# Message products with stationary weights, turned by VectorE, in a graph network layer on one Trainium2 core

## The chip, the cores and the metric

The kernel runs on one core of one Trainium2 chip. A core has five engines that run their own instruction streams: PE (matrix products), DVE (vector), ACT (activations), POOL (here it issues the gathers) and SP (here it issues other transfers). The metric is the device time of one execution in microseconds; lower is better. The kernel before took 5120.48 us, the median of 3 runs (5115.68 to 5129.49).

## The reference

One layer of a graph network with N = 12500 nodes, C = 96 channels and E = 412500 edges that have 4 attributes each. The edges come sorted by dst.

```python
def _mlp(h, W, b, gamma, beta):
    h = jax.nn.relu(h @ W + b)
    mu = jnp.mean(h, axis=0)
    var = jnp.mean(jnp.square(h - mu), axis=0)
    return gamma * (h - mu) * jax.lax.rsqrt(var + EPS) + beta

node_feat = _mlp(x, W_node, ...)
edge_feat = _mlp(edge_attr, W_edge, ...)
message = jnp.concatenate([x[row], x[col], edge_feat], axis=1)   # row = src, col = dst
message = _mlp(message, W_msg, ...)
agg = segment_sum(message, col, N)
out = _layernorm(x + agg + node_feat)
```

The norm of the messages is over all edges, so that the kernel needs, of the relu'd messages h, the sums by dst (with a count), the total and the total of squares; it applies the norm to the sums at the end.

## The kernel before, in words

The product with W_msg is split by its three parts. x @ W_src and x @ W_dst are computed once per node into two tables in DRAM, p_tab and q_tab (tables(), L180). A message is then relu(p_tab[src] + q_tab[dst] + edge part).

Edges are taken in tiles of 128 (one edge a partition), groups of GT = 4 tiles (512 edges) and blocks of BG = 4 groups (16 tiles). There are NT = 3223 tiles, NG = 806 groups and NBL = 202 blocks. As the edges are sorted by dst, the edges of a group fall on few nodes: a window of WN = 31 nodes, and the windows of the four groups of a block start WS = 16 nodes apart, so that a block covers NW - 1 = 79 nodes.

**Gathers.** gather() (L202) issues one indirect DMA per tile on POOL: 128 rows of 96 floats from p_tab, by src. In the first stages, in which tables, node MLP and the statistics of the edge norm are computed, POOL gathers the rows of the first 29 blocks ("early" ones) and SP writes them to DRAM (spill, blocks(), L217). The other 173 blocks ("late" ones) are gathered in the main loop, through a ring of 7 tiles of two groups each (RING = 14 groups); ahead_of() issues the four gathers of the group 14 ahead, and its tile comes free when the message() of the groups in it has read it. plan() (L91) mixes the blocks: about every sixth late block is followed by an early one, whose rows SP fetches back (fetch(), L572) and which needs no gather.

**The main loop** (L704 to L780, about 900 to 5066 us of the execution) goes over the groups k in that order. All its engines' orders are written out by hand: an engine executes what the loop names in the order of the loop. For a group:

- edges() (L599): a bf16 product of 512 columns with the edge attributes (split in bf16 parts) and, for the place of an edge in its window, a one-hot condition, into the PSUM tile pr, two groups at a time.
- prepare() (L608): ACT takes the relu of both groups (127 partitions x 1024) into left. left has for each edge, a column, 96 edge features, 31 rows that select the node in the window, and a row of ones.
- linear() (L615): for each of the 4 tiles, a fp32 product with 128 columns of left as the stationary side and rhs (96 rows of weights, 31 rows of q_tab, the bias; 96 columns) as the moving one. The result z has an edge a partition, 96 columns, and lies in one of three PSUM banks zb (ZB = 3).
- message() (L627): DVE adds the gathered rows to z, and takes the relu, into h (128 x 384).
- squared() (L648): ACT squares two groups of h; moments() (L653) adds them on DVE into the PSUM tile mixed.
- places_of() (L639): once per block DVE compares the place of each edge with the 31 numbers of its group's window; the result, at, is the one-hot of 128 edges x 80 places (the 80th column is one, for the total).
- sums() (L672): per tile, a fp32 product with h (97 columns) stationary and the 80 columns of at moving, added up over a block in one of two PSUM banks by_place.
- add() (L695): DVE adds the bank to total and to agg at the block's first node, a block and 2 groups later.

An fp32 product shows in the trace as two weight loads (PEld) and two matmuls (PE). linear() works up to ZB - 1 = 2 groups ahead of message(), sums() LATER = 2 groups behind. Behind the loop come the statistics and the output (to 5104 us).

Of the kernel before, what the change touches and what calls it, by code (L numbers as in the profile page):

```python
# [26 lines left out]
P = 128  # L27
# [13 lines left out]
RW = 7  # L41
# [27 lines left out]
AB, HP, RB, ZB = 2, 3, 3, 3  # L69
NW = WS * (BG - 1) + WN + 1  # L70
OW = NW * GT + WS * (BG - 1)
# [36 lines left out]
def gnn(ctx, tc, t):  # L108
# [35 lines left out]
    iota = const.tile([P, BG, WN], F32, name="iota")  # L144
    nc.gpsimd.iota(iota, pattern=[[WS, BG], [1, WN]], base=-WM, channel_multiplier=0,
# [123 lines left out]
    with tc.tile_pool(name="win", bufs=1) as win, tc.tile_pool(name="win_ps", bufs=2, space=PSUM) as ps:  # L269
# [12 lines left out]
        worst = win.tile([P, 2, BG], F32, name="worst")  # L282
        for k in range(BG):
            nc.vector.tensor_reduce(worst[:, 0, k:k + 1], rel[:, k:NG:BG, :], axis=AX.XY, op=OP.max)
            nc.vector.tensor_reduce(worst[:, 1, k:k + 1], rel[:, k:NG:BG, :], axis=AX.XY, op=OP.min)
        out = win.tile([P, 1], F32, name="out")
        nc.vector.tensor_sub(worst[:, 0, :], worst[:, 0, :], iota[:, :, WN - 1])
        nc.vector.tensor_sub(worst[:, 1, :], iota[:, :, 0], worst[:, 1, :])
        nc.vector.tensor_reduce(out, worst.rearrange("p a k -> p (a k)"), axis=AX.X, op=OP.max)
# [29 lines left out]
    def places():  # L319

        with tc.tile_pool(name="lin", bufs=2) as work, tc.tile_pool(name="lin1", bufs=1) as one:
            first = one.tile([P, RW], I32, name="first")
            nc.sync.dma_start(first, t["first"])
            rows = [stack_d[HI + BG * i:HI + BG * (i + 1), :].rearrange("g (c b e) -> (g c) b e", b=RW, e=GE)
# [151 lines left out]
    def fast(ring):  # L476
        y0s, pair = [], [None]

        def ahead_of(g):
            if g % 2 == 0:  # L480
                pair[0] = ring.tile([P, 2, GT, C], F32, name="pg")
            if g < NG:
                return gather(g, pair[0][:, g % 2, :, :])

        with tc.manual_schedule(engines={ET.SP, ET.Pool}):
# [23 lines left out]
            got = {g: ahead_of(g) for g in range(SPILL, SPILL + RING)}  # L509
        with tc.tile_pool(name="fix", bufs=1) as fix, tc.tile_pool(name="msg", bufs=2) as work, \  # L510
                tc.tile_pool(name="msg_ps", bufs=2, space=PSUM) as ps:
            squares = fix.tile([P, C], F32, name="squares")
            mixed = ps.tile([P, GE], F32, name="mixed", bufs=1)
            wide_sq = mixed[:, :GT * C].rearrange("p (t c) -> p t c", c=C)
            nc.vector.memset(wide_sq, 0.0)
            nodes_of = mixed[:, GT * C:GT * C + BG * WN].rearrange("p (k w) -> p k w", w=WN)
            nc.vector.tensor_copy(nodes_of, iota)
            by_place = [ps.tile([P, GE], F32, name=f"pa{i}", bufs=1) for i in range(2)]
# [15 lines left out]

            at = [fix.tile([P, BG, OW], F32, name=f"at{i}") for i in range(AB)]
            for x in at:
                nc.vector.memset(x, 0.0)
                for i in range(BG):
                    o = WS * (BG - 1 - i)
                    nc.vector.memset(x[:, i, o:o + NW * GT].rearrange("p (t w) -> p t w", w=NW)[:, :, NW - 1:], 1.0)  # L540


            zb = [ps.tile([P, GE], F32, name=f"z{i}", bufs=1) for i in range(ZB)]
# [7 lines left out]
            def load(s):  # L551
# [16 lines left out]
                rows = bass.AP(rows.tensor, rows.offset, [[C, WN], [WS * C, BG], [1, C]], None, rows.runtime_checks)  # L568
# [3 lines left out]
            def fetch(s):  # L572
                b = order[s]
                if b * BG < SPILL:
                    back = work.tile([P, BG, GT, C], F32, name="pb", bufs=1)
                    nc.sync.dma_start(back, spill[b].rearrange("p g (a c) -> p g a c", a=GT))
                    for i in range(BG):
                        got[b * BG + i] = back[:, i, :, :]

            def unread(n):  # L580
                busy = ps.tile([P, 2, GE], F32, name="pr", bufs=1)[:, 0, :GE // 2]
                for i in range(n):
                    nc.tensor.matmul(busy, ident[:C], big[:C, -GE // 2:], start=True, stop=True)

            raw = {}

            def transposed(k):

                s, g = steps[k]
                px = ps.tile([P, 2, GE], F32, name="pr", bufs=1)  # L590
                for i in range(2):
                    for t in range(GT):
                        nc.tensor.transpose(px[:C, i, t * P:(t + 1) * P], got[g + i][:, t, :], ident)  # L593
                xt = work.tile([C, 2, GE], F32, name="xt", bufs=1)
                nc.scalar.activation(xt, px[:C], AF.Copy)  # L595
                for i in range(2):
                    raw[g + i] = xt[:, i, :]

            def edges(s, half):  # L599

                n = min(2, NG - order[s] * BG - 2 * half)
                if n > 0:
                    prs[s, half] = ps.tile([P, 2, GE], F32, name="pr", bufs=1)
                for i in range(n):
                    nc.tensor.matmul(prs[s, half][:, i, :], we[:, 2 * half + i, :], block[s],  # L605
                                     start=True, stop=True)

            def prepare(s, half):  # L608

                n = min(2, NG - order[s] * BG - 2 * half)  # L610
                if n > 0:
                    pr, x = prs.pop((s, half)), left[s % 2]
                    nc.scalar.activation(x[:C + WN, 2 * half:2 * half + n, :], pr[:C + WN, :n, :], AF.Relu)  # L613

            def linear(k):  # L615
                s, g = steps[k]
                n = min(GT, NT - g * GT)
                for i in range(n):
                    nc.tensor.matmul(zb[k % ZB][:, i * C:(i + 1) * C],  # L619
                                     left[s % 2][:KR, g % BG, i * P:(i + 1) * P],  # L620
                                     rhs[:KR, s % RB, g % BG, :], start=True,
                                     stop=g not in raw)
                    if g in raw:
                        nc.tensor.matmul(zb[k % ZB][:, i * C:(i + 1) * C], raw[g][:, i * P:(i + 1) * P],  # L624
                                         w_msg[:, 0, :], start=False, stop=True)

            def message(k):  # L627
                s, g = steps[k]
                n = min(GT, NT - g * GT)
                z = zb[k % ZB][:, :n * C].rearrange("p (t c) -> p t c", c=C)  # L630
                h = hb[k // 2 % HP][:, k % 2, :, :C]
                rows = got.pop(g)
                if g in raw:
                    nc.vector.tensor_scalar(h, z, 0.0, MOST, op0=OP.max, op1=OP.min)
                    return
                nc.vector._custom_dve(TENSOR_ADD_SAT, out=h[:, :n, :], in0=z, in1=rows[:, :n, :],  # L636
                                      s0=MOST, s1=0.0)

            def places_of(s):  # L639

                b = order[s] * BG
                o, m = WS * (BG - 1), min(BG, NG - b)
                to = at[s % AB][:, :m, o:o + NW * GT].rearrange("p g (t w) -> p g t w", w=NW)[:, :, :, :WN]
                nc.vector.tensor_tensor(  # L644
                    to, rel[:, b:b + m, :].unsqueeze(3).to_broadcast([P, m, GT, WN]),
                    nodes_of[:, :m].unsqueeze(2).to_broadcast([P, m, GT, WN]), op=OP.is_equal)

            def squared(k, m=2, n=GT):  # L648
                sq = work.tile([P, 2, GT, C], F32, name="sq")
                nc.scalar.activation(sq[:, :m, :n, :], hb[k // 2 % HP][:, k % 2:k % 2 + m, :n, :C], AF.Square)  # L650
                return sq

# [7 lines left out]
            def collect(x, n, r=P):  # L660

                plus = nc.gpsimd.tensor_add
                whole = n if r == P else n - 1
                if r < P:
                    plus(squares[:r], x[:r, whole * C:n * C], squares[:r])
                while whole > 1:
                    half = whole // 2
                    plus(x[:, :half * C], x[:, :half * C], x[:, (whole - half) * C:whole * C])
                    whole -= half
                plus(squares, x[:, :C], squares)  # L670

            def sums(k):  # L672
# [4 lines left out]
                o = WS * (BG - 1 - i)  # L677
                for t in range(n):
                    r = min(P, E - (g * GT + t) * P)
                    nc.tensor.matmul(by_place[s % 2][:C + 1, :NW], hb[k // 2 % HP][:r, k % 2, t, :],  # L680
                                     at[s % AB][:r, i, o + NW * t:o + NW * (t + 1)],
# [13 lines left out]
            def add(s, val):  # L695

                pt = by_place[s % 2][:C + 1, :NW]
# [7 lines left out]
            with tc.manual_schedule(engines={ET.SP, ET.Pool, ET.PE, ET.DVE, ET.Activation}):  # L705
                bad = nc.values_load(flag, min_val=0, max_val=1, skip_runtime_bounds_check_because="a comparison's result")
                load(0)
                fetch(0)
                load(1)
                fetch(1)  # L710
                for half in range(2):
                    edges(0, half)
                    prepare(0, half)
                edges(1, 0)
                for k in range(ZB - 1):
                    linear(k)
                places_of(0)
                waiting, last = None, BG * (len(order) - 1)
                for k in range(last):
                    s, g = steps[k]  # L720
                    if g % BG == 0:
                        if s + 2 < len(order):
                            load(s + 2)
                            fetch(s + 2)
# [320 lines left out]
```

## Time and profile before

| | |
|---|---|
| median of 3 runs | 5120.48 us |
| the profiled execution: its time, its span | 5105.89 us, 5104.1 us |
| mean granted clock of TensorE | 0.66 |
| the main loop | about 900 to 5066 us |
| largest group of ACT in the loop: relu, L613 | 403 x 1021 ns, 411.4 us |
| DMA traffic over the span | 317.20 MB, 62 GB/s |

The page of the profile gives each engine's busy time, a chart of 40 slices, the DMA queues, the chain that ended last and the costliest groups of instructions. A line such as `L613 ACT ACTIVATE left<-pr 127x1024 f32<-127x1024 f32 x403 | 411.4, 1021 | 2696.3 <-remote 2114.7` has the kernel's line, engine, operation, output and input with their shapes (partitions x elements), and the count; then the busy time of all and the mean duration of one in ns; then the idle time of the engine just before them, and what ended most of it. "issue" is time in which an engine waited for nothing that the profile shows. Of 40 slices, these show that from the seventh on the loop is even:

```profile
PE   3244443445555555555555655555555555555656
DVE  1457767222222222222222222222222222222224
POOL 4755555655556656666565666665666666656664
PEclk6557666666666666666666666666666666666667
```

### The profile page before, as it was taken

How to read it: one execution, taken by the hardware profiler on the slowest of the kernel's cores; microseconds unless marked ns; L12 is line 12 of the kernel's file. 1: busy time of each engine (PE TensorE's matmuls, PEld its weight loads, DVE VectorE, ACT ScalarE, POOL GpSimd, SP SyncE). 2: the span in 40 equal slices, each digit the busy share in tenths (PEclk: the TensorE clock that was granted, in tenths of full speed). 3: DMA queues.
4: the chain of work that ended last, by engine and by line, in shares of the span. 5: the costliest groups of instructions: out<-in, count | busy, mean ns of one | idle time of the engine just before them, and what ended most of it. 6: DMA issues, size and time to landing. Idle time of an engine off the chain costs nothing.

```text
span 5104.1 us, 43293 instructions
## 1 busy us (share of the span) xinstructions
PE 2651.1 (52%) x15169; PEld 2168.5 (42%) x15169; DVE 1575.8 (31%) x3039; ACT 1138.2 (22%) x1226; POOL 3088.9 (61%) x3248
## 2 busy tenths in 40 slices
PE   3244443445555555555555655555555555555656
PEld 3031111445444444444444544445444444444545
DVE  1457767222222222222222222222222222222224
ACT  0426554111111111111111211112111111111112
POOL 4755555655556656666565666665666666656664
PEclk6557666666666666666666666666666666666667
DMA  6734443221222222222222212222212222212122
GB/s 162 248 113 95 101 98 92 49 48 48 59 56 47 46 46 49 46 48 49 46 46 46 48 39 48 47 50 47 47 46 47 49 46 47 48 45 48 40 47 59
DMA packets 214865, 317.20 MB, mean 62 GB/s; under 512 B 126498, under 2 KB 132988, under 8 KB 211808
## 3 DMA queue, kind: packets, MB, share of 16 engines
q0 software_dynamic: 103040, 158.48, 14.7%
q1 hardware_dynamic: 98635, 150.92, 10.0%
q10 hardware_dynamic: 12960, 4.93, 0.4%
q8 instruction: 122, 2.00, 0.2%
q14 instruction: 108, 0.88, 0.1%
HBM read 258.19 MB, written 55.89 MB: 62 GB/s over the span
## 4 chain that ended last, share of the span: by engine, by line
PE 34%; issue 27%; another core or an unknown queue 17%; ACT 3%; DVE 2%; ACTq 0%; DVEq 0%
PE z L619 17%; PE pa L680 12%; PE pr L605 5%; ACT left L613 2%; ACT sq L650 1%; DVE estats L409 0%; DVE part L414 0%; PE z L624 0%; DVE h L636 0%; PE pr L593 0%; DVE y L968 0%; ACT xt L595 0%; DVE sd L971 0%; ACT sq L970 0%
## 5 line engine op out<-in xcount | busy, mean ns | idle before, releaser
L207 POOL DMA_INDIRECT pg<-p_tab,src x3156 | 3005.8, 952 | 1902.8 <-issue 893.4
L619 PE MATMUL z<-rhs,left 128*128 128x96 f32 x6446 | 1224.8, 323 | 788.0 <-issue 784.1
L619 PEld LDWEIGHTS z<-rhs,left 128*128 128x128 f32 x6446 | 1127.7, 240 | 929.1 <-issue 877.6
L680 PE MATMUL pa<-at,h 128*97 128x80 f32 x6446 | 1006.2, 287 | 948.9 <-issue 944.8
L680 PEld LDWEIGHTS pa<-at,h 128*97 128x97 f32 x6446 | 873.5, 205 | 1066.9 <-issue 1065.8
L636 DVE CUSTOM_DVE_ANT_0 h<-z,pg 128x384 f32<-128x384 f32 x690 | 376.0, 554 | 2673.7 <-remote 2149.2
L613 ACT ACTIVATE left<-pr 127x1024 f32<-127x1024 f32 x403 | 411.4, 1021 | 2696.3 <-remote 2114.7
L650 ACT ACTIVATE sq<-h 128x768 f32<-128x768 f32 x404 | 339.6, 840 | 725.7 <-DVE h L636 385.1
L656 DVE TENSOR_TENSOR mixed<-mixed,sq 128x384 f32<-128x384 f32 x802 | 450.0, 561 | 13.9
L409 DVE BATCH_NORM_STATS2 estats<-r 128x6 f32<-128x512 f32 x606 | 364.8, 678 | 130.7 <-issue 85.1
L403 PE MATMUL pr<-ea,wide 128*128 128x512 bf16 x606 | 227.1, 494 | 261.1 <-issue 107.4
L407 ACT ACTIVATE r<-pr 128x1024 f32<-128x1024 f32 x303 | 296.8, 1036 | 260.8 <-PE pr L403 119.5
L605 PE MATMUL pr<-late,we 128*128 128x512 bf16 x690 | 270.9, 472 | 107.8 <-issue 54.7
L403 PEld LDWEIGHTS <-wide 128*128 128x128 bf16 x606 | 68.0, 114 | 420.0 <-issue 374.1
L636 DVE CUSTOM_DVE_ANT_0 h<-z,pb 128x384 f32<-128x384 f32 x100 | 54.4, 555 | 365.6 <-remote 284.5
L605 PEld LDWEIGHTS <-we 128*128 128x128 bf16 x806 | 89.8, 122 | 175.5 <-issue 175.2
L644 DVE TENSOR_TENSOR at<-rel,mixed 128x496 f32<-128x496 bf16 x202 | 135.2, 669 | 7.2 <-issue 0.4
L373 PE MATMUL py<-center,big 96*128 96x96 f32 x196 | 44.0, 425 | 135.2 <-ACT big L368 101.1
L373 PEld LDWEIGHTS py<-center,big 96*128 96x128 f32 x196 | 42.3, 331 | 137.0 <-ACT big L368 101.4
L207 POOL DMA_INDIRECT pg<-in_x,src_raw x64 | 61.3, 958 | 64.6 <-DMA spill<-pg 44.2
L191 PE MATMUL pt<-w_msg,big 96*128 96x192 f32 x196 | 42.6, 388 | 62.4 <-issue 39.3
L191 PEld LDWEIGHTS pt<-w_msg,big 96*128 96x128 f32 x196 | 40.6, 233 | 64.0 <-issue 44.9
(126 smaller groups left out, 624.3 us busy)
## 6 DMA issues: line engine op xcount, KB each, us to landing
pg<-p_tab,src POOLq DMA_INDIRECT x3156
pb<-spill SPq DMA_DIRECT2D x29, 768.0 KB
spill<-pg SPq DMA_DIRECT2D x55, 384.0 KB
ea<-stack_d SPq DMA_DIRECT2D x25, 480.0 KB
stack_d<-y SPq DMA_DIRECT2D x24, 448.0 KB
late<-stack_d SPq DMA_DIRECT2D x57, 180.0 KB
rhs<-q_tab SPq DMA_DIRECT2D x202, 46.5 KB
x<-in_ea SPq DMA_DIRECT2D x8, 896.0 KB
```

Source lines behind the costliest of these rows:

```text
L207: made = [nc.gpsimd.indirect_dma_start(out=pg[:, i, :], out_offset=None, in_=tab[:, :], in_offset=bass.IndirectOffsetOnAxis(ap=idx[:, i:i ...
L403: nc.tensor.matmul(pr[:, k % 2, :], wide[:, P * i:P * (i + 1)], ea[:, b % J, :], start=True, stop=True)
L407: nc.scalar.activation(r, pr, AF.Relu)
L409: nc.vector.bn_stats(stats[:, (k - o) % NS, (k - o) // NS, :], r[:, 1 - o, :])
L605: nc.tensor.matmul(prs[s, half][:, i, :], we[:, 2 * half + i, :], block[s], start=True, stop=True)
L613: nc.scalar.activation(x[:C + WN, 2 * half:2 * half + n, :], pr[:C + WN, :n, :], AF.Relu)
L619: nc.tensor.matmul(zb[k % ZB][:, i * C:(i + 1) * C], left[s % 2][:KR, g % BG, i * P:(i + 1) * P], rhs[:KR, s % RB, g % BG, :], start=True, ...
L636: nc.vector._custom_dve(TENSOR_ADD_SAT, out=h[:, :n, :], in0=z, in1=rows[:, :n, :], s0=MOST, s1=0.0)
L644: nc.vector.tensor_tensor(to, rel[:, b:b + m, :].unsqueeze(3).to_broadcast([P, m, GT, WN]), nodes_of[:, :m].unsqueeze(2).to_broadcast([P, ...
L650: nc.scalar.activation(sq[:, :m, :n, :], hb[k // 2 % HP][:, k % 2:k % 2 + m, :n, :C], AF.Square)
L656: nc.vector.tensor_tensor(wide_sq, wide_sq, sq[:, i, :, :], op=OP.add)
L680: nc.tensor.matmul(by_place[s % 2][:C + 1, :NW], hb[k // 2 % HP][:r, k % 2, t, :], at[s % AB][:r, i, o + NW * t:o + NW * (t + 1)], start=i ...
```

## The change

Products of the messages have rhs stationary and the 512 columns of left moving, so that a group is one fp32 product and z comes out transposed, 96 channels x 512 edges, in one of two PSUM banks zt. by_edge(), new, turns it on DVE: the three quarters of 32 channels each are transposed in 32x32 blocks (one instruction per quarter, 32 partitions x 512), from zt into z, which takes three of the four banks of mixed and holds the whole block. An instruction turns blocks in place of the 32 partitions, so that group i of a block gets the partitions 32 i to 32 i + 31 of all 16 tiles: the host deals the edges to tiles anew (a quarter of 32 edges from each group), and each tile then covers all 79 places of the block. So places_of() compares 79 numbers for each of 16 tiles. message() does two groups' worth, 768 columns, at a time. There is one bank of sums, so that add() of a block comes ahead of the sums of the next. pr is one bank; edges() and prepare() work by the group. The order of a block is written out anew. The last block, with fewer edges, has a window spacing of 7 (LS) and shorter columns, and the end of the loop is adapted; the check that all edges fall into their windows goes by quarters, with bounds from the host. The path for other inputs (general()) gets the old deal of the edges as inputs of its own. At the end, the squares of the last tiles are taken tile by tile.

The core of the diff:

```diff
-AB, HP, RB, ZB = 2, 3, 3, 3
+AB, HP, RB, ZB = 2, 3, 3, 2
...
-            mixed = ps.tile([P, GE], F32, name="mixed", bufs=1)
-            wide_sq = mixed[:, :GT * C].rearrange("p (t c) -> p t c", c=C)
+            mixed = ps.tile([P, 4 * GE], F32, name="mixed", bufs=1)
+            z = mixed[:, :BT * C].rearrange("p (t c) -> p t c", c=C)
+            wide_sq = mixed[:, BT * C:(BT + GT) * C].rearrange("p (t c) -> p t c", c=C)
...
-            by_place = [ps.tile([P, GE], F32, name=f"pa{i}", bufs=1) for i in range(2)]
+            by_place = ps.tile([P, GE], F32, name="pa", bufs=1)
...
-            at = [fix.tile([P, BG, OW], F32, name=f"at{i}") for i in range(AB)]
+            at = [fix.tile([P, BT, NW], F32, name=f"at{i}") for i in range(AB)]
...
-            zb = [ps.tile([P, GE], F32, name=f"z{i}", bufs=1) for i in range(ZB)]
+            zt = [ps.tile([P, GE], F32, name=f"z{i}", bufs=1) for i in range(ZB)]
...
+            def linear(s, i):
+
+                n, raw = columns(s), order[s] < RAW
+                nc.tensor.matmul(zt[i % ZB][:C, :n], rhs[:KR, s % RB, i, :], left[s % 2][:KR, i, :n],
+                                 start=True, stop=not raw)
...
+            def by_edge(s, i):
+
+                n = columns(s)
+                for q in range(C // QE):
+                    nc.vector.transpose(z[i * QE:(i + 1) * QE, :n // QE, q * QE:(q + 1) * QE],
+                                        zt[i % ZB][q * QE:(q + 1) * QE, :n].rearrange("p (t e) -> p t e", e=QE))
+
+            def message(k, m=2, n=2 * GT):
...
+                o = k % 2 * GT
+                zg = z[:, g % BG * GT:g % BG * GT + n, :]
+                h = hb[k // 2 % HP].rearrange("p m t c -> p (m t) c")[:, o:o + n, :C]
...
+                rows = got[g // 2 * 2].rearrange("p m t c -> p (m t) c")[:, o:o + n, :]
+                nc.vector._custom_dve(TENSOR_ADD_SAT, out=h, in0=zg, in1=rows, s0=MOST, s1=0.0)
...
+                nc.vector.tensor_tensor(
+                    at[s % AB][:, :m, :NW - 1],
+                    rel.rearrange("p g t -> p (g t)")[:, order[s] * BT:order[s] * BT + m].unsqueeze(2)
+                    .to_broadcast([P, m, NW - 1]),
+                    nodes_of.unsqueeze(1).to_broadcast([P, m, NW - 1]), op=OP.is_equal)
...
-                    nc.tensor.matmul(by_place[s % 2][:C + 1, :NW], hb[k // 2 % HP][:r, k % 2, t, :],
-                                     at[s % AB][:r, i, o + NW * t:o + NW * (t + 1)],
+                    nc.tensor.matmul(by_place[:C + 1, :NW], hb[k // 2 % HP][:r, k % 2, t, :],
+                                     at[s % AB][:r, i * GT + t, :],
...
+                for s in range(len(order) - 1):
+                    k, late_ = s * BG, order[s] * BG >= SPILL
+                    if s + 3 < len(order):
+                        load(s + 3)
+                    if s + 2 < len(order):
+                        fetch(s + 2)
+                    for i in range(2):
+                        linear(s + 1, i)
+                    for half in range(2):
+                        message(k + 2 * half)
+                        if late_:
+                            for _ in range(2):
+                                ahead_of(ahead)
+                                ahead += 1
+                        now = squared(k + 2 * half)
+                        if half == 0:
+                            if waiting:
+                                moments(waiting, False)
+                            places_of(s + 1)
+                            for i in range(2):
+                                if s + 2 < len(order):
+                                    edges(s + 2, i)
+                                    prepare(s + 2, i)
+                                sums(k + i)
+                        else:
+                            sums(k + 2)
+                            for i in range(BG):
+                                if i >= 2:
+                                    linear(s + 1, i)
+                                by_edge(s + 1, i)
+                            for i in range(2, BG):
+                                if s + 2 < len(order):
+                                    edges(s + 2, i)
+                                    prepare(s + 2, i)
+                            sums(k + 3)
+                            moments(waiting, s == len(order) - 2)
+                            add(s, place(s))
...
+                        waiting = now
```

More of the change, by code (lines that the diff above doesn't have):

```diff
@@ L599, in edges @@
[L599 to L634, printed above, removed]
+                    nc.tensor.matmul(busy[:, :P], ident, ident, start=True, stop=True)
+            def columns(s):
+                return GE if order[s] < NBL - 1 else LE
@@ L706, in fast @@
                 bad = nc.values_load(flag, min_val=0, max_val=1, skip_runtime_bounds_check_because="a comparison's result")
[L707 to L716, printed above, removed]
+                for s in range(3):
+                    load(s)
```

225 lines of the change are left out of this document (118 added, 107 removed).

## The prediction, made before the change was run

> **What bounds the kernel now.** I read the page from top to bottom first, then the waits, then the main loop alone by windows, and last single stretches of PE and POOL in the timeline. The page's totals name no engine:
>
> ```profile
> span 5104.1 us, 43293 instructions
> PE 2651.1 (52%) x15169; PEld 2168.5 (42%) x15169; DVE 1575.8 (31%) x3039; ACT 1138.2 (22%) x1226; POOL 3088.9 (61%) x3248
> L207 POOL DMA_INDIRECT pg<-p_tab,src x3156 | 3005.8, 952 | 1902.8 <-issue 893.4
> ```
>
> POOL, which issues the gathers, is the busiest at 61%. What it waits for stands in the waits, and beside it what PE does meanwhile:
>
> ```profile
> DVE h L636 <- remote: 2433.7, 242, 21.5
> POOL pg L207 <- DVE h L636: 800.2, 139, 19.3
> PE z L619 <- issue: 784.1, 824, 2.5
> PE pa L680 <- issue: 944.8, 910, 2.5
> ```
>
> Columns: total us, times, longest. POOL stops 139 times for the message on DVE, because a ring tile comes free only when message() has read it. And PE stands about 1730 us at "issue", which is to say waiting for nothing that the profile shows. The loop and one cycle of it:
>
> ```profile
> 950.00:5040.00 4090.00, 2227.91 (x13521) 1933.03 (x13521) 997.24 (x2155) 727.78 (x792) 2522.11 (x2674) 0.66 0.21 47
> ...
> 5046.00:5061.00 15.00, 15.00 (x152) 14.71 (x152) 10.67 (x24) 6.67 (x8) 2.24 (x4) 1.00 0.01 1
> 2516.00:2534.00 18.00, 3.15 (x11) 2.34 (x12) 2.49 (x6) 0.84 (x1) 13.73 (x15) 0.61 0.32 87
> ...
> 2615.60:2646.40 30.80, 13.41 (x84) 11.99 (x84) 6.46 (x14) 4.35 (x5) 22.63 (x24) 0.67 0.20 44
> ...
> 2539.60:2560.30 20.70, 13.24 (x81) 10.97 (x80) 4.19 (x10) 3.47 (x4) 15.01 (x16) 0.66 0.26 57
> ```
>
> ```profile
> 2504.43 0.94 POOL L207 DMA_INDIRECT pg<-p_tab,src  x1 [5.16 <-DVE h L636]
> ...
> 2533.12 0.94 POOL L207 DMA_INDIRECT pg<-p_tab,src  x1 [0.30 <-issue]
> 2539.51 0.94 POOL L207 DMA_INDIRECT pg<-p_tab,src  x1 [5.45 <-DVE h L636]
> ...
> 2558.24 0.94 POOL L207 DMA_INDIRECT pg<-p_tab,src  x1 [0.30 <-issue]
> 2562.92 0.94 POOL L207 DMA_INDIRECT pg<-p_tab,src  x1 [3.74 <-DVE h L636]
> ```
>
> ```profile
> 2522.76 0.32 PE L619 MATMUL z<-rhs,left 128*128 128x96 f32 x1 [2.48 <-issue]
> 2524.86 0.32 PE L619 MATMUL z<-rhs,left 128*128 128x96 f32 x1 [1.78 <-issue]
> ...
> 2536.76 0.46 PE L680 MATMUL pa<-at,h 128*97 128x80 f32 x2 [1.80 <-issue]
> 2537.46 0.45 PE L680 MATMUL pa<-at,h 128*97 128x80 f32 x1 [0.25 <-issue]
> 2538.16 2.02 PE L619 MATMUL z<-rhs,left 128*128 128x96 f32 x8 [0.25 <-issue]
> ...
> 2544.47 1.07 PE L619 MATMUL z<-rhs,left 128*128 128x96 f32 x8
> ```
>
> ```profile
> 2661.43 0.38 PE L605 MATMUL pr<-early,we 128*128 128x512 bf16 x1 [0.71 <-issue]
> 2662.46 0.38 PE L605 MATMUL pr<-early,we 128*128 128x512 bf16 x1 [0.66 <-issue]
> ```
>
> In the windows the columns are length, then busy us and (instructions) of PE, PEld, DVE, ACT, POOL, and the clock. The reader is to see a cycle. POOL issues a gather each (2533.12-2504.43)/23 = 1.247 us. While it does, PE executes some 150 instructions at full speed and then drips: 23 in the 18 us from 2516, a fifth of the 8 weight loads and 8 matmuls that it does in 1.07 us at 2544. A drip costs the same for 96 columns (about 2 us a pair at 2522) or fewer as for 512 (1.03 us a pair at 2661): it counts instructions, not columns. Then z is late, message() is late, no ring tile comes free, POOL stops at 2534, and some 3 us later (2537 to 2538) PE is at full speed again; the message runs and POOL resumes. In the last stretch from 5046, without new gathers, PE is dense at clock 1.00.
>
> So a run of POOL gives PE a budget: 161 instructions in a window of 20.7 us, 168 in one of 30.8; in between 0.7 per us. The idle time that it costs: 4090 - 2674 x 1.247 = 755 us, 5.4 for each of 139 pauses. That is what this change can win or lose; with no pause left the loop couldn't be shorter than POOL's 3335 us.
>
> The Trainium skill has another reading of a slow PE ("TensorE: Matmul & The Clock Gate", Part 1): a PE that has idled for a window of about 3.4 us gets half its clock. The trace shows such halves (2.02 against 1.07 us for the same eight at 2538 and 2544), but half a clock doesn't open gaps of 2 us between single instructions. By the clock alone POOL would never have been stopped.
>
> **The change, part by part.**
>
> *PE's instructions.* A block of 16 tiles has 16 x 4 for z, 16 x 4 for the sums and 4 x 2 for the edges: 136. The change turns z into 4 matmuls of 512 columns, 16 instructions: 88 per block. The time of the dense ones hardly moves: z of a group took 1.07 us warm, and two passes of 512 fp32 columns are near it by the next row, 2 x 0.72 with overlap. So only the count matters.
>
> *DVE.* Rows for its part:
>
> ```profile
> L636 DVE CUSTOM_DVE_ANT_0 h<-z,pg 128x384 f32<-128x384 f32 x690 | 376.0, 554 | 2673.7 <-remote 2149.2
> L656 DVE TENSOR_TENSOR mixed<-mixed,sq 128x384 f32<-128x384 f32 x802 | 450.0, 561 | 13.9
> L644 DVE TENSOR_TENSOR at<-rel,mixed 128x496 f32<-128x496 bf16 x202 | 135.2, 669 | 7.2 <-issue 0.4
> L409 DVE BATCH_NORM_STATS2 estats<-r 128x6 f32<-128x512 f32 x606 | 364.8, 678 | 130.7 <-issue 85.1
> L377 DVE COPY y0s<-py 128x768 f32<-128x768 f32 x12 | 11.2, 950 | 41.8 <-remote 28.8 <-PE py L373 13.0
> L700 DVE TENSOR_TENSOR agg<-pa,agg 97x79 f32 x202 | 46.7, 231 | 0.0
> L699 DVE TENSOR_TENSOR total<-pa,total 97x1 f32<-97x1 f32 x202 | 30.8, 153 | 5.1 <-PE pa L776 3.6 <-PE pa L680 0.7
> L359 PE MATMUL pn<-big,w_node 96*96 96x512 f32 x48 | 26.7, 719 | 3.6 <-ACT agg L360 3.2 <-DVE most L293 0.4
> ```
>
> Before, a block costs 4 x 0.554 + 4 x 0.561 + 0.669 + 0.384 = 5.5 us. After: two messages of 768 columns at 0.95 (a copy as wide), 1.9; moments as before, 2.24; places_of 1264 columns instead of 496, 0.669 + 768 x 1.03 ns (the slope between 384 and 768) = 1.46; add 0.38; and twelve turns. No row has a turn. Its bounds are 0.554 us (384 columns) and 1.11 (each column passed twice); I take 0.678, the row with the same 512 columns: 8.1 us. Sum 14.1, and about 1 us of waits for z^T between the turns, since two banks hold four groups: 15 us.
>
> The Trainium skill speaks against the turns ("VectorE: DVE Perf Modes", Two Vector instructions with no wait between them): an instruction whose input starts in another quadrant of partitions than the last one's is held until all earlier ones have finished. Each turn of a group does. No row here shows the price; the upper bound would stand for it.
>
> *Order.* Now message(k) needs all turns of its block, and on DVE it stands behind moments and behind add(s), which waits for the last sums of the block before. So one block is a chain of about 15 us: sums, turns, sums, moments, add, message. Nothing of it overlaps the next. Both pair tiles of a block come free close together, as between message(k) and message(k+2) stand only moments and places_of (2.6 us). One bank of sums adds that add(s) is queued ahead of everything else of the next block on DVE, and PE's next sums behind add(s). It is covered while POOL has ring tiles to fill: a block's gathers are 16 x 1.247 = 20 us.
>
> *ACT, edges.* Four relus of half the width: off the chain. Host order, the bounds check and the row spacings move nothing on the chip that isn't beside the early gathers: 0, at most 1 us.
>
> **The sum.** Between pauses POOL runs for whole blocks. Two blocks take 40 us and need 2 x 88 = 176 instructions; the budget at 42 us (run and what remains of its pause) is 161 + 0.7 x 21 = 176. It is on the edge, so I take half of the runs to end after two and half after three. In a run of three the budget at 62 us is 190 of 264: 74 of a block's 88 are left when POOL stops, and are done at the chain's speed, 74/88 x 15 = 12 us, with 3 us until PE is dense again: a pause of 15. A run of two leaves a few instructions: 5 us, like now. The 2674 gathers are 167 blocks, so 33 pairs of such runs: 33 x 20 = 668 us. The 29 early blocks take 88 instructions each and free no ring tile; between nothing (within the budget) and 15 us, I take 10: 290. Idle time 958 against 755: +204. Behind the last gather (5035) the ring's 3.5 blocks are drained at 15 us each, 52 us; now the sums end 30 us behind it, between these two rows:
>
> ```profile
> 5035.15 0.95 POOL L207 DMA_INDIRECT pg<-p_tab,src  x1 [0.30 <-issue]
> ```
>
> ```profile
> 5064.45 0.64 PE L583 MATMUL pr<-big,ident 96*128 96x256 f32 x2
> ```
>
> That is +22. The profiled execution took 5105.9 us (span 5104.1), which is 0.3% below the median of the three runs, 5120.5. The sum goes by the first: 5106 + 204 + 22 = 5332, taken as **5330**, 4% slower. Own range: with turns at 0.554 the chain is 13.5 us, the pauses 33 x 18.5 and the early blocks 9 each, 5240; with all runs of three, 56 x 15 + 290 = 1130, 5500.
>
> **Rivals.**
>
> *All runs end after two blocks* (a few instructions more of budget than three windows showed): 83 x 5 + 290 = 705 idle, -50 + 22: 5080. For it: the budget is on the edge. Against: the ring also carries an error of one block on.
>
> *Faster: the count alone decides.* The chain hides beside the gathers, since 15 us is under POOL's 20, and the pauses shrink with the instructions: 755 x 88/136 = 489, with the tail 5106 - 266 + 22 = 4862. For it: pauses are set by PE's budget, and 64% of the instructions need fewer. Against: once POOL has stopped, what is left of a block was some 2 us of PE work and is now 15 us of chain.
>
> *DVE becomes the bound.* With a turn at 1.11 a block costs 20 us, no less than its gathers: pauses (3 + 74/88 x 20 = 20, and 6), 33 x 26 + 29 x 14 = 1264, +509, tail +40: 5655. It decides from a turn of about 1.05 us.
>
> *Nothing moves*: the pauses are set by something that neither count nor chain touches, 5106. Against it: POOL's releaser in the waits is DVE's message, and the stretch before it is PE's.
>
> **How the numbers follow.** Chances: the sum 0.47; all runs of two 0.12; the count alone 0.28; DVE 0.08; nothing 0.05. The kernel's runs differ by 0.3%, which is what a measurement of it can tell. Two-block runs (5080, 0.5% under) I divide by 0.08 and 0.03 to faster and same, and 0.01 to slower. Faster 0.28 + 0.08 = 0.36; same 0.03 + 0.05 = 0.08; slower 0.47 + 0.08 + 0.01 = 0.56. The range reaches from the count alone to near DVE as bound: 4850 to 5600.
>
> **What would show it.** Right, if the loop shows 88 PE instructions per block, drips at the same pace, fewer and longer pauses of POOL (about 65 of 15 or 5 us, with early ones), a turn near 0.68 us and DVE near 14 us per block. The count alone is right if the pauses are fewer and no longer than now. The sum is wrong if PE no longer drips, if the budget counts something else (with z at 512 columns, the same number of pauses per block), or if the last gather comes before 4900.

## The result, and the profile after

The changed kernel took 5857.15 us (median of 4 runs, 5852.53 to 5862.22) beside 5118.33 us of the kernel before: ratio 1.1439, 95% interval 1.1419 to 1.1459. The direction was forecast; the size was not: 5330 was forecast, and 5857 lies above the range. The profiled execution took 5858.7 us against 5105.9, 753 more.

The page of the profile, its head and the groups that answer to those shown before:

```profile
span 5856.9 us, 36348 instructions
...
PE 2793.7 (48%) x10245; PEld 1474.2 (25%) x10245; DVE 3461.8 (59%) x5053; ACT 1197.6 (20%) x1641; POOL 3086.9 (53%) x3248
...
L210 POOL DMA_INDIRECT pg<-p_tab,src x3156 | 3004.3, 952 | 2643.1 <-DVE h L644 1457.4
L631 DVE STREAM_TRANSPOSE mixed<-z 32x512 f32<-32x512 f32 x2424 | 1765.7, 728 | 1929.5 <-remote 1577.2
...
L644 DVE CUSTOM_DVE_ANT_0 h<-mixed,pg 128x768 f32<-128x768 f32 x346 | 327.2, 946 | 0.0
...
L650 DVE TENSOR_TENSOR at<-rel,mixed 128x1264 f32<-128x1264 bf16 x202 | 296.2, 1467 | 7.3 <-DVE early L557 0.5
```

Instructions fell by a sixth and no engine is near full. POOL's gathers cost the same 3004 us; its idle time grew. The waits (total us, times, longest):

```profile
ACT left L616 <- remote: 1996.9, 143, 21.1
DVE mixed L631 <- remote: 1577.2, 147, 21.6
POOL pg L210 <- DVE h L644: 1457.4, 87, 35.9
```

POOL stops 87 times instead of 139, and nearly doubles what it loses. One cycle, from the middle of a run of gathers, which began at 2472.64, to the first gather of the next (time, duration, and in brackets the idle time before it and who ended it):

```profile
2489.00 0.58 PE L611 MATMUL pr<-early,we 128*128 128x512 bf16 x1
...
2496.57 2.25 DVE L631 STREAM_TRANSPOSE mixed<-z 32x512 f32<-32x512 f32 x3 [2.77 <-remote]
...
2498.67 0.60 ACT L616 ACTIVATE left<-pr 127x512 f32<-127x512 f32 x1 [9.92 <-remote]
...
2499.32 0.58 PE L611 MATMUL pr<-early,we 128*128 128x512 bf16 x1 [9.06 <-issue]
...
2502.27 2.29 PE L621 MATMUL z<-left,rhs 128*96 128x512 f32 x4
...
2511.34 0.94 POOL L210 DMA_INDIRECT pg<-p_tab,src  x1 [0.30 <-issue]
2516.87 0.60 ACT L616 ACTIVATE left<-pr 127x512 f32<-127x512 f32 x1 [17.60 <-remote]
...
2517.51 0.58 PE L611 MATMUL pr<-early,we 128*128 128x512 bf16 x1 [12.96 <-ACT left L616]
...
2517.75 4.65 DVE L631 STREAM_TRANSPOSE mixed<-z 32x512 f32<-32x512 f32 x6 [18.94 <-remote]
...
2523.80 0.94 DVE L644 CUSTOM_DVE_ANT_0 h<-mixed,pg 128x768 f32<-128x768 f32 x1
...
2525.01 0.94 POOL L210 DMA_INDIRECT pg<-p_tab,src  x1 [12.72 <-DVE h L644]
```

This is the cycle to read. The product for the edges is recorded at 2499.32 and lasts 0.58 us; the relu that reads it starts at 2516.87, 17 us behind its end, and ACT ran nothing in the 17.60 us before it. The z products are recorded until 2504.56; their turns start at 2517.75, 13 us later. "remote" says the same: the semaphore arrived long after the recorded end of the instruction that raises it (the trace has its update at 2516.84). DVE's signal to POOL doesn't lag: the message ends at 2524.74 and POOL's gather starts at 2525.01. So **PE's results come late**, and the last ones come in some 4.5 us after POOL's last gather (2511.34 + 0.94). Then what is left of DVE's chain runs, 8 us, and POOL resumes after 12.5 us.

In these two kernels, how late goes with how many PE instructions (weight loads and matmuls) were recorded since POOL resumed. I worked the table out of the records: the median of the relu's start minus the end of the product it reads, for products during a run of POOL (a count can have few products: the changed kernel has one at 70 to 79, the kernel before twelve at 80 to 89):

```
PE instructions since      kernel before            changed kernel
POOL resumed            late by   at us in run   late by   at us in run
0 to 39                 0.04 us   1 to 2         0.04 us   1 to 9
50 to 59                0.32      5              0.04      11
70 to 79                3.5       6              6.4       16
80 to 89                9.8       7              9.4       16
100 to 109              10.7      6              17.7      27
110 to 129              25        8 to 9         -         -
```

The two kernels reach the 65th instruction at different times, 5 and over 11 us into the run, and the lateness sets in at about the same count. Behind it two instructions took about 2 us in the cycle above: the turns at 2496.57 read the z product just ahead of the edge product of 2489.00, and the relu at 2498.67 reads that edge product, a weight load and a matmul further on. The result after that, at 2516.84, gives no pace, as it came in with POOL's stop.

The sum of the difference: POOL's pauses in the loop 747 us before and 1473 after, +726; from the last gather to the last sums 30 and 46 us, +16; the rest, about 10 us, ahead of 950 us.

### The profile page after: what moved, and what is told of

It reads as the page before. It is cut to its first block, busy times and chain, and to the rows that moved or that the text cites. A ratio compares the mean times of both kernels' runs of the same rounds, so it can differ in the third digit from the quotient of the medians.

```text
span 5856.9 us, 36348 instructions
## 1 busy us (share of the span) xinstructions
PE 2793.7 (48%) x10245; PEld 1474.2 (25%) x10245; DVE 3461.8 (59%) x5053; ACT 1197.6 (20%) x1641; POOL 3086.9 (53%) x3248
## 4 chain that ended last, share of the span: by engine, by line
DVE 41%; another core or an unknown queue 30%; issue 12%; PE 4%; SPq 2%; DMA 2%; ACT 1%; DVEq 1%; ACTq 0%
DVE mixed L631 27%; DVE h L644 6%; DVE mixed L669 6%; PE z L621 1%; SPq L461 1%; DMA ea<-stack_d 1%; PE pa L688 1%; DMA erow<-p_tab 1%; DVE at L650 1%; ACT left L616 1%; DVE estats L419 0%; DVE total L707 0%; DVE agg L708 0%; PE pr L413 0%
## 5 line engine op out<-in xcount | busy, mean ns | idle before, releaser
L631 DVE STREAM_TRANSPOSE mixed<-z 32x512 f32<-32x512 f32 x2424 | 1765.7, 728 | 1929.5 <-remote 1577.2
L621 PE MATMUL z<-left,rhs 128*96 128x512 f32 (+1 forms) x1616 | 1279.5, 913 | 255.9 <-DVE mixed L631 242.1
L688 PEld LDWEIGHTS pa<-at,h 128*97 128x97 f32 x6446 | 890.6, 219 | 1479.3 <-issue 1130.6
L611 PE MATMUL pr<-late,we 128*128 128x512 bf16 x692 | 350.2, 506 | 1752.4 <-ACT left L616 1077.9
L616 ACT ACTIVATE left<-pr 127x512 f32<-127x512 f32 (+1 forms) x808 | 479.6, 594 | 3165.5 <-remote 1996.9
L688 PE MATMUL pa<-at,h 128*97 128x80 f32 x6446 | 913.2, 304 | 193.8 <-DVE h L644 168.2
L621 PEld LDWEIGHTS z<-left,rhs 128*96 128x96 f32 x1616 | 333.6, 247 | 753.5 <-DVE mixed L631 498.8
L644 DVE CUSTOM_DVE_ANT_0 h<-mixed,pg 128x768 f32<-128x768 f32 x346 | 327.2, 946 | 0.0
L650 DVE TENSOR_TENSOR at<-rel,mixed 128x1264 f32<-128x1264 bf16 x202 | 296.2, 1467 | 7.3 <-DVE early L557 0.5
L611 PE MATMUL pr<-early,we 128*128 128x512 bf16 x116 | 59.2, 510 | 250.2 <-ACT left L616 145.1
```

What stands on the lines that cost most here:

```text
L611: nc.tensor.matmul(prs[s, i][:, :n], we[:, i, :], block[s][:, :n], start=True, stop=True)
L616: nc.scalar.activation(left[s % 2][:C + WN, i, :n], prs.pop((s, i))[:C + WN, :n], AF.Relu)
L621: nc.tensor.matmul(zt[i % ZB][:C, :n], rhs[:KR, s % RB, i, :], left[s % 2][:KR, i, :n], start=True, stop=not raw)
L631: nc.vector.transpose(z[i * QE:(i + 1) * QE, :n // QE, q * QE:(q + 1) * QE], zt[i % ZB][q * QE:(q + 1) * QE, :n].rearrange("p (t e) -> p t ...
L644: nc.vector._custom_dve(TENSOR_ADD_SAT, out=h, in0=zg, in1=rows, s0=MOST, s1=0.0)
L650: nc.vector.tensor_tensor(at[s % AB][:, :m, :NW - 1], rel.rearrange("p g t -> p (g t)")[:, order[s] * BT:order[s] * BT + m].unsqueeze(2) . ...
```

## The experiments

Two theories. Theory A: where PE's results come late, the change is slow because a block became a chain of hand-overs from PE to ACT and DVE. Theory B, the rival: DVE's chain of 15 us a block costs the time by itself.

**No gathers, z in pieces, no turns, another order.** Four kernels, run beside each other, each an edit of the changed kernel. The first leaves out the gathers of the main loop and reads the rows of 14 groups again and again (its expectation says 12); the third leaves out most of the turns.

```diff
# e1_no_gathers
-                                ahead_of(ahead)
+                                got[ahead // 2 * 2] = got[SPILL + (ahead - SPILL) // 2 * 2 % RING]
# e2_z_in_pieces
+                    for o in range(0, n, P):
+                        nc.tensor.matmul(zt[i % ZB][:C, o:o + P], rhs[:KR, s % RB, i, :],
+                                         left[s % 2][:KR, i, o:o + P], start=True, stop=True)
# e3_no_turns
+                if 4 <= s < len(order) - 2:
+                    return
# e4_turns_first, the order of a block
 linear(s + 1, 0), linear(s + 1, 1)
 message(k), message(k + 2)
 by_edge(s + 1, 0), by_edge(s + 1, 1), linear and by_edge (s + 1, 2), linear and by_edge (s + 1, 3)
 add(s - 1), places_of(s + 1)
 edges(s + 2, i), prepare(s + 2, i) for 4 i
 sums(k), sums(k + 1), sums(k + 2), sums(k + 3), moments of both halves
```

> Leaves out the gathers of the main loop: the late blocks read the rows of the first 12 groups that were gathered ahead of it, again and again. Theory A (late results): while POOL gathers, PE's results are reported late, nothing for the first 65 instructions or so since POOL resumed and then about 0.95 us for each instruction in PE's queue; the block's chain of hand-overs from PE to ACT and DVE is stretched by that. Without gathers a block is DVE's chain alone, 15.5 us, and the kernel about 900 + 201 x 15.5 + 60 = 4080 us, with no result later than 1 us. Theory B (the chain of 15 us on DVE by itself, whatever PE does) gives the same 4080 here. A PE that is slow for a reason of its own (its clock, the 512-column products) would keep the loop near 5000 and the total above 5000.

> linear() makes the 512 columns in four products of 128: the same columns and turns, but 64 PE instructions for z in a block instead of 16, 136 in all as before the change. Theory A: 48 more instructions a block at up to 0.95 us each behind the 65th: runs of POOL fall back to one block, with a pause of 10 to 14 us each, 500 to 1000 us longer, 6350 to 6850. Theory B: PE's dense time grows by little and is beside DVE's chain: within 60 us of 5857.

> Leaves out the turns of all blocks but the first four and the last two (message() adds the rows to an old z). Theory A: the late results stay; of a pause only the 6 turns in it go (4.7 us) and the waits of z for a bank: 87 pauses x 5 = 430 us, about 5400, still slower than the kernel before. Theory B: with DVE's chain at 6 us a block the pauses shrink to those of the kernel before or less, 4900 to 5100.

> Another order: both messages of a block, then at once all turns of the next block, and only then the edges, the sums and the moments; add() of a block comes behind the next block's turns; four buffers for h. DVE's work is the same. Theory A: 24 PE instructions instead of 88 stand between a block's messages and the last turns of the next one; a run of two blocks needs 112 instructions of about 100 that are reported in 40 us, so its pause falls from 16 us to 6 to 9: 87 x 8 = 700 us less, 5150 (5000 to 5350). Theory B: a block still costs DVE 15 us in a row: 5750 to 5857.

Measured: 3905.8, 4130.7, 4130.6 and 4152.6 us. But the kernel before took 4137.63 us beside them, not 5118. None of the expectations for late results could be tested, because in these executions none were late. What they did show is DVE's chain alone, in the run without gathers:

```profile
2499.73 9.35 DVE L631 STREAM_TRANSPOSE mixed<-z 32x512 f32<-32x512 f32 x12
...
2515.17 9.35 DVE L631 STREAM_TRANSPOSE mixed<-z 32x512 f32<-32x512 f32 x12
```

That is 15.4 us a block, where the sum of the prediction had 15. The kernel without gathers came 174 us below the 4080 that both theories gave it: their 900 us for the first stages were about 200 fewer here (the first message runs at 709 us). Theory B failed on the spot: it gave 5750 to 5857 for the turns first and 4900 to 5100 without turns.

**The two kernels as they are, again.**

> The changed kernel as it is. In the four runs before this one no result of PE was late and POOL never stopped, and the kernel before took 4138 us instead of 5118: the late results belong to some executions' chip, not to the kernel. Theory A (the change costs time only where PE's results are late): where the kernel before takes about 4138, POOL's gathers bound both kernels and this one takes 4130 to 4160; where it takes about 5118, this one takes about 5857 again. Theory B (DVE's chain of 15 us a block costs the time by itself): longer than the kernel before by 10% or more on either.

> The kernel before as it is, for its profile on the same chip as the run ahead of it. Theory A: where it takes about 4138 us, PE's instructions don't drip, no relu starts over 1 us after the product that it reads, and POOL stops at most a few times; where it takes about 5118, all three are as in the first profile. Theory B says nothing of it.

Here results were late: 5877.6 us beside 5190.5, ratio 1.132 (1.1298 to 1.1342). Both profiles are like the first ones: the relu of the kernel before waits 2311.5 us for "remote", the lateness sets in at about the same count (1.7 us at 50 to 59, 9.2 at 70 to 79), and the changed kernel has the same 89 pauses in the loop, 78 of them after 32 gathers.

**The four edits again.**

> The kernel of e1 again, in the hope of a chip on which PE's results are late (the kernel before at 5100 to 5200 us beside it). Theory A, there: without gathers no result is late, and the kernel takes what it took in e1, 3906, within 1%. If PE's results were late there for a reason other than POOL's gathers, it would take over 4500. On a chip without late results: 3906.

> The kernel of e2 again (z in pieces of 128 columns, 136 PE instructions a block). Theory A, where results are late: each piece counts against the same allowance, so longer than the changed kernel by 500 to 1000 us, 6350 to 6850. Theory B (DVE's chain by itself): within 60 us of 5870. On a chip without late results: 4130.

> The kernel of e3 again (no turns). Theory A, where results are late: PE's queue is as long as in the changed kernel, and only DVE's part of a pause goes, about 5 us of each of 87: about 5400, above the kernel before. Theory B: pauses as in the kernel before or less, 4900 to 5100. On a chip without late results: 4130.

> The kernel of e4 again (turns ahead of the sums). Theory A, where results are late: 24 instead of 88 PE instructions between a block's messages and the next block's last turns, pauses of 6 to 9 us instead of 16 after two blocks: 5150 (5000 to 5350). Theory B: 5750 to 5870. On a chip without late results: 4150.

3907.4, 4149.5, 4130.2 and 4153.8 us, the kernel before 4121.8: again no late results.

**The changed kernel where nothing is late.**

> The changed kernel as it is, once more. Theory A: on a chip where the kernel before takes 4120 to 4140, POOL never stops and this one takes 4120 to 4160, no change; where that takes 5100 to 5200, about 5870. Theory B: 10% or more longer on either.

> The kernel of e4 once more (turns ahead of the sums). Theory A, where results are late: 24 instead of 88 PE instructions between a block's messages and the next block's last turns, 5150 (5000 to 5350). Theory B: 5750 to 5870. On a chip without late results: 4150.

4146.6 us beside 4137.2, ratio 1.0031 (1.0014 to 1.0048), and 4152.5. This rules theory B out: the same turns, the same 15 us chain, and no cost beyond 0.3%. Of theory A it shows the condition, that the cost needs late results, and not yet why it is as large as it is. The changed kernel's head and groups in this run:

```profile
span 4151.4 us, 36348 instructions
...
PE 2714.5 (65%) x10245; PEld 1388.7 (33%) x10245; DVE 3463.6 (83%) x5053; ACT 1218.5 (29%) x1641; POOL 3092.9 (75%) x3248
...
POOL pg L210 28%; DVE mixed L631 18%; DVE estats L419 9%; DMA pg<-p_tab,src 8%; DVE h L644 4%; DVE mixed L669 3%; PE z L621 2%; PE py L978 1%; DMA q_tab<-trow 1%; DVE at L650 1%; PE py L383 1%; PE pt L194 0%; PE pr L611 0%; PE pa L688 0%; DVE part L424 0%
...
L210 POOL DMA_INDIRECT pg<-p_tab,src x3156 | 3010.2, 954 | 995.9 <-issue 880.7
L631 DVE STREAM_TRANSPOSE mixed<-z 32x512 f32<-32x512 f32 x2424 | 1765.7, 728 | 169.0 <-PE z L624 15.6
```

DVE is busy 83% where it was 59%, the turns' idle time is 169 us instead of 1930, POOL leads the chain, and in the waits no "remote" is left; in their place stands this:

```profile
DVE h L644 <- DMA pg<-p_tab,src: 251.2, 69, 5.2
```

Now the messages wait for the gathered rows, the other way round. POOL never stops in the loop.

**Pieces and order where results are late.** In the first of the next two runs nothing was late, in the second results were.

> Turns ahead of the sums, as in e4. Theory A, where results are late: 5150 (5000 to 5350), with pauses of 6 to 9 us after runs of two blocks. If the pauses are set by the number of PE instructions in a run and not by where the turns stand in PE's queue: 5750 to 5870 as with the changed order. On a chip without late results: 4150.

4160.6 us beside 4137.9: no answer.

> z in pieces of 128 columns, as in e2. Theory A, where results are late: 48 more PE instructions a block behind the same allowance of about 65, 500 to 1000 us longer than the changed kernel, 6350 to 6850. If the pauses come from DVE's chain and PE's place in it alone, not from the count: within 60 us of 5870. On a chip without late results: 4130 to 4150.

5596.0 us, the kernel before 5168.5: late results, and theory A's number was wrong in sign. With 48 more PE instructions a block the kernel was 280 us *shorter* than the changed kernel in its second late measurement (5877.6), 1.083 times the kernel before against 1.132. This is one run. The windows of the loop, changed kernel first, then the pieces:

```profile
950.00:5720.00 4770.00, 2342.83 (x8676) 1245.13 (x8676) 2817.14 (x4093) 778.83 (x1186) 2501.88 (x2652) 0.67 0.18 40
```

```profile
950.00:5440.00 4490.00, 2625.76 (x13177) 2226.20 (x13175) 2825.49 (x4070) 778.43 (x1178) 2490.54 (x2637) 0.63 0.18 43
```

PE does half as many instructions again in less time, for the same work of DVE, ACT and POOL. A cycle of the pieces shows where it stops:

```profile
2499.70 0.74 DVE L636 STREAM_TRANSPOSE mixed<-z 32x512 f32<-32x512 f32 x1
...
2499.88 1.48 PE L693 MATMUL pa<-at,h 128*97 128x80 f32 x8
...
2504.35 0.38 PE L611 MATMUL pr<-late,we 128*128 128x512 bf16 x1
...
2508.79 0.16 DVE L712 TENSOR_TENSOR total<-pa,total 97x1 f32<-97x1 f32 x1 [7.08 <-remote]
2508.92 0.24 DVE L713 TENSOR_TENSOR agg<-pa,agg 97x79 f32 x1
2509.09 0.96 DVE L649 CUSTOM_DVE_ANT_0 h<-mixed,pg 128x768 f32<-128x768 f32 x1
...
2510.32 0.95 POOL L210 DMA_INDIRECT pg<-p_tab,src  x1 [4.65 <-DVE h L649]
```

The late result that ends the wait is here that of the last sums, recorded until 2501.36, for add() at 2508.79. The turns of the next block were done at 2500.44, and 1.3 us after the start of add() the message is out. The pauses of POOL in the loop, counted from its records (gathers in the run ahead of the pause; the typical pause is the median):

```
kernel           pauses   after 16           after 24          after 32           idle time
before           140      67, 3.5 us         62, 4.9 us        -                  747 us
changed           89      10, 15.4 us        -                 78, 12.5 us        1473
z in pieces      167      166, 4.3 us        -                 -                  1205
```

With 136 instructions a block the first block of a run isn't through in 20 us, so all runs but one hold one block: 167 short pauses. With 88 the first block's messages are out in time (at 2486.86 and 2490.51 in the cycle of the changed kernel, 14 and 18 us into the run), POOL goes on, and the second block is caught half way, with its last turns late: half as many pauses, of 16.6 us on average instead of 7.2. On this reading, an instruction saved bought a longer run and a worse place to stop.

The count alone doesn't set the lateness either. With z in pieces, products at 80 to 89 instructions were late by 1.6 us (median of 265), where the table has 9.8 for the kernel before and 9.4 for the changed kernel; at 90 to 99 by 3.6. What else enters is open.

**The order, where results are late: no answer.** Three more runs of the turns-first kernel, and one that also dropped the gathers from the 140th block on:

> Turns ahead of the sums, as in e4. The run with z in pieces showed that what a block costs is how many blocks a run of POOL holds: with 136 PE instructions a block each run held one block and the pause was 5 us; the changed kernel's runs hold two, and the pause is 16. Theory A, where results are late: the last turns stand behind 24 instead of 88 PE instructions; two blocks a run with a pause of 6 to 9 us, 5150 (5000 to 5350). Theory C (the late results of the whole queue must come in before POOL goes on, wherever the turns stand, since the next block's z stands behind this block's sums): 26 us a block as now, 5750 to 5900. On a chip without late results: 4150.

> As for the run before: where PE's results are late, theory A 5150 (5000 to 5350) with pauses of 6 to 9 us after two blocks; theory C 5750 to 5900, 26 us a block as in the changed kernel. On a chip without late results: 4150 to 4165.

> As for the two runs before: where PE's results are late, theory A 5150 (5000 to 5350), pauses of 6 to 9 us after two blocks; theory C 5750 to 5900, 26 us a block as in the changed kernel. On a chip without late results: 4150 to 4165.

> Turns first, as in e4, and from the 140th block on no gathers (the rows of the last 14 groups are read again and again). Where PE's results are late: theory A for the first 140 blocks 20 to 22 us a block, pauses of 6 to 9 us after two blocks, theory C 26 us a block; in the last 60 blocks no late result and 15 us a block if POOL's gathers are what makes them late, 20 us or more if not. On a chip without late results: 3334 gathers' time gone only in the last third, 17 us a block first and 15 us then, about 4050.

4162.5, 4154.8, 4151.4 and 4108.9 us (4050 was expected of the last), the kernel before 4137 to 4145: nothing was late in any. Whether the turns would be better ahead of the sums, and whether the lateness ends without gathers in an execution that has it, stays open. That the gathers cause it is argued from the lateness setting in behind POOL's resuming and ending 4 to 5 us behind its last gather, in five profiles, and isn't shown by taking them away. There is a rival that no run touches: each of these executions was recorded by the profiler, and whether results would come late without the recording is open.

## Why the prediction was wrong

**What bounds the kernel.** Right: the loop is POOL's gathers plus its pauses, and a pause ends with DVE's message. Wrong: what PE's drip is. I read it as PE executing 161 instructions in a window and so having done them. The drip is a late symptom. Results come late from about the 65th instruction on, and PE's records run on ahead of that: in the kernel before, the first 140 since POOL resumed take 10.5 us (median) and the next ten another 3.7, which is where the drip begins. In the changed kernel the records stop for another reason, as the next product waits for ACT (12.96 us at 2517.51). The sign stood in the quoted row "DVE h L636 <- remote: 2433.7": the wait ended with a semaphore that arrived far behind its instruction. I took it for z being late. The reading that a drip costs the same for any number of columns wasn't borne out by its own rows either: about 2 us a pair at 96 columns and 1.03 at 512.

**PE's instructions, DVE's work, the tail.** Right: 88 instructions a block, dense z unchanged, and each DVE row near its value (forecast in brackets): message 0.946 (0.95), places_of 1.467 (1.46), turn 0.728 (0.678), the block 15.4 us (15), the tail +16 (+22). The turns cost 9.35 us between start and end of twelve against 8.1: (9.35 - 0.728) / 11 = 0.784 us from start to start, more than the 0.728 that one lasts, and far from the bound of 1.11. Before the change two messages of 0.554 took 1.02 us together, so those overlapped a little. That the turns don't overlap agrees with the Trainium skill ("VectorE: DVE Perf Modes", Two Vector instructions with no wait between them), by which such instructions are held.

**The sum.** The step that failed is "A run of two leaves a few instructions: 5 us, like now." 78 of 89 runs held two blocks, the second case of the sum, and their pause was 12.5 us: 4.5 us until late results are in, and 8 us of chain behind them (six turns, moments, add, message). No run held three, so the half of the runs that the sum gave to three was wrong too. A two-block run left far more than a few instructions to wait for, because their results, though recorded, had not come in. The measured pauses: 68 of 12.8 us on average, 873, and 21 of 28.5 us, 599, in each of which an early block's two messages lie. So the early blocks added 21 x 15.7 = 330, where I had 290, and the pauses themselves 89 x 12.8 = 1140, where I had 668. The difference between 958 and 1473 is nearly all in the second. What makes the results late stays open.

**The direction.** Slower was forecast and came, but this hung on the kind of execution, of which the prediction knew nothing: where no result was late, the change cost 0.3%, near its rival "nothing moves".

**The rivals.** "All runs end after two blocks" was the right count with the wrong price, 5080 for 5857. "The count alone decides" fell: the changed kernel has fewer instructions than the kernel before and is slower, and the pieces, with the old count, were 280 us shorter than the changed kernel. "DVE becomes the bound" is out: DVE is busy 59% of the span, and where nothing is late the same turns cost 0.3% at most. The clock as the reason for slow PE stays out: the granted clock was 0.66 before and 0.67 after, the products were recorded, and it is their results that were late.

## What to carry to other kernels

Look at the time from the end of a producer to the start of its consumer, not only at when the producer runs: a wait marked "remote" is a result that arrived late. Count not only how often an engine stops but what is left of the chain when it does: here 89 pauses of 16.6 us cost more than 167 of 7.2 or 140 of 5.3, so that fewer instructions were worse. And measure a change on more than one occasion: the same two kernels stood 14% apart on one and 0.3% on another.

## What was not expected of the hardware

The kernel before took 4122 to 4145 us on five chips and 5118 to 5190 on other occasions, evenly each time. One chip showed both, so that neither the kernel nor the chip alone decides. POOL starts a gather every 1.25 us in both. In the long kind PE's results lag by up to 25 us while POOL gathers (and the first stages are longer: the first message of the changed kernel runs at 925 us instead of 708); in the short kind no wait for "remote" is left. What differs between them is not shown by any row here.
